# Expert units of two mixture-of-experts layers as side work of the state space block between them

## The chip, the cores and the metric

The kernel runs on one NeuronCore of a Trainium2 chip. The core has TensorE (PE, with its weight loads shown as PEld), VectorE (DVE), ScalarE (ACT), GpSimd (POOL) and SyncE (SP), each with its own in-order stream of instructions, and 16 DMA engines. The metric is device time in microseconds, the median of repeated runs; one further execution is profiled.

## The reference

4096 tokens of width 256 (two sequences of 2048) pass through three residual steps: a half-weighted expert layer, a state space block, and the same expert layer again.

```python
x = x + 0.5 * ffn(layernorm(x))      # 8 experts, top 2, capacity 640 per choice
x = x + attn(layernorm(x))           # Mamba block, then a squared-ReLU MLP
x = x + 0.5 * ffn(layernorm(x))      # the same weights again
```

The expert layer routes every token to its two best experts out of eight. For each of the two choices a token's position in its expert's queue is the running count over all tokens before it, and positions from 640 on are dropped. The expert is two matrix products (256 to 1024, ReLU, 1024 to 256), and the result is weighted by the gate probability and added to the token.

The Mamba block projects to 512 channels, convolves over four tokens, and then runs the recurrence `h = h*exp(dt*A) + dt*u*B` with 16 states for each channel along all 2048 tokens. Its output is `y = sum over states of h*C, plus x_conv*D`, multiplied by `silu(z)` and projected back to 256. All of it is float32.

## The kernel before

**Three stages one after the other.** `moe1` (L697) routes all 32 token tiles of 128 in five groups (`route`, L303), stores the normalized rows with their two gates in DRAM (`self.rows`), and copies x to `self.acc`. `experts` (L684) stores the list of token numbers per expert (`store_list`, L495), cuts every expert's kept tokens into units of 256 slots (`plan`, L504), and runs 32 of these (`units`, L570). If the plan holds more than 32, a branch runs seven more. `mamba` (L1095) is the middle stage, and `moe2` (L726) is `experts` again on the block's output, whose routing was done inside the middle stage.

**A unit.** It fetches 256 token numbers, then their rows, by indirect DMA on POOL's queue (L589, L600), and the expert's weights (L609) unless the buffer three units back holds the same expert. PE transposes the rows (4 transposes, L621), runs 16 matmuls into the hidden layer (L640, 256 columns each) and 16 out of it (L656). ACT does ReLU with bias, DVE adds the second bias and multiplies by the gate, and two indirect DMAs add the 256 rows to `acc` or `out` (L662).

**The middle stage.** The tokens are cut in 8 chunks of 512, the channels in 4 blocks of 128, taken in 2 pairs. `recurrence` (L928) is a hand-written order of 8 x 2 x 16 x 2 = 512 slots (chunk, pair, state, block of the pair). In a slot ACT makes the decay (`dA`, L969), DVE scans 512 tokens (L979) and multiplies by C (L989), and PE adds the product into `y_ps` by a matmul with the identity (L994). POOL makes the input term `db` for both blocks of a pair at once (L961, 128x1024). B and C rows come broadcast by DMA (`bt`, `ct`, L949 and L950), one pair ahead. After the 16 states of a pair, `gate` (L996) adds x_conv*D on DVE (L1002) and multiplies by silu(z) on POOL (L1006).

**Side chains.** What a chunk needs before its slots (`chunk_front`, L735: norm, projections, convolution, softplus) and after them (`chunk_tail`, L1026: projection out, MLP, dispatch to experts) are Python generators. Each `yield Need(...)` announces the next step with a cost for each engine, a PSUM bank, and marks to wait for. `Side` (L70) keeps a running clock of each engine's work; after each slot it puts in those steps that fit (`slot`, L141), and before a step of the main order that needs a mark it forces the steps that lead to it (`until`, L155). All of it is decided when the program is built; on the chip each engine runs its stream in that order.

Of the kernel before, what the change touches and what calls it, by code (L numbers as in the profile page):

```python
# [35 lines left out]
NU = K2 * NT // UN  # L36
MU = NU + E - 1
NWB = 3
W_2 = ND * FF
W_B1 = W_2 + NF * D  # L40
W_B2 = W_B1 + NF
# [9 lines left out]
XB = 4  # L51
PR = 2
NP = NC // PR
GROUPS = (4, 4, 8, 8, 8)
# [3 lines left out]
class Need:  # L58
# [4 lines left out]
    def __init__(self, pe=0.0, act=0.0, dve=0.0, pool=0.0, bank=0, free=0, after=None, sets=None):  # L63
        us = {"pe": pe, "act": act, "dve": dve, "pool": pool}
        self.us = {e: t for e, t in us.items() if t}
        self.bank, self.free, self.sets = int(bank), free, sets
        self.after = None if after is None or after[1] < 0 else after


class Side:  # L70
# [6 lines left out]
    OWN = {"dve": 1.8, "act": 0.88, "pe": 0.88, "pool": 1.25}  # L77
# [9 lines left out]
    def begin(self, chain, at=0.0):  # L87
        self.chains.append([chain, None, at])
        self.advance(self.chains[-1])
# [9 lines left out]
    def advance(self, chain):  # L99
        need = next(chain[0], None)  # L100
        while need is not None and not isinstance(need, Need):
            self.begin(need, chain[2])
            need = next(chain[0], None)
        chain[1] = need
        if need is None:
            self.chains.remove(chain)

# [9 lines left out]
    def step(self, chain):  # L117
# [8 lines left out]
        if need.sets:  # L126
            self.mark(need.sets, end)
# [27 lines left out]
    def until(self, mark):  # L155

        while mark[1] >= 0 and mark not in self.marks:
            self.step(min(filter(self.may, self.chains), key=lambda c: self.start(c)[1]))


class Kernel:
# [6 lines left out]
    def setup(self):  # L168
        nc, ins = self.nc, self.ins
        cp = self.ctx.enter_context(self.tc.tile_pool(name="const", bufs=1))  # L170
        self.cpool = self.ctx.enter_context(self.tc.tile_pool(name="count", bufs=2))
        dp = self.ctx.enter_context(self.tc.tile_pool(name="scratch", bufs=1, space=DRAM))
# [32 lines left out]
        self.need = const([P, K2 * CAP // UN], "need")  # L205
        nc.gpsimd.iota(self.need, pattern=[[UN, K2 * CAP // UN]], base=0, channel_multiplier=0,
# [29 lines left out]
        none = const([1, 1], "none_i", I32)  # L236
        nc.gpsimd.memset(none, NT)

# [24 lines left out]
        for c in range(NC):  # L263
            for k in range(DC):
                nc.vector.tensor_scalar_mul(
                    self.taps[:, c, k, :], self.ident, self.half[:, c, k : k + 1]
                )
        self.minus = const([P, 1], "minus")
# [12 lines left out]
        self.rows = dp.tile([NT + 1, RW], F32, tag="rows", name="rows")  # L281
        row = const([1, RW], "none")
        nc.gpsimd.memset(row, 0.0)
        nc.sync.dma_start(out=self.rows[NT:, :], in_=row)
        self.lists = [dp.tile([NULL + 1, 1], I32, tag=f"list{i}", name="lists") for i in range(2)]
        for t in self.lists:
            nc.sync.dma_start(out=t[NULL:, :], in_=none)
# [15 lines left out]
    def route(self, x, t0, pool, bank):  # L303

        nc = self.nc
        n = x.shape[1]
        W, W3, Q = [P, n, E], [P, n, K2], K2 * E
        num = self.exp_m8.unsqueeze(1).to_broadcast(W)

        def t(name, shape=W, dtype=F32, **kw):  # L310
            return pool.tile(shape, dtype, tag=f"r_{name}", name=name, **kw)
# [25 lines left out]
        lg = t("lg")  # L337
        for j0 in range(0, n, 4):
# [22 lines left out]
            for j in range(4):  # L361
# [5 lines left out]
                lg[:, j0 : j0 + 4, :], lq, self.gb.unsqueeze(1).to_broadcast([P, 4, E]), ALU.add  # L367
            )

# [50 lines left out]
        g1 = row[:, :, D]  # L420
        nc.vector.scalar_tensor_tensor(g1, e2, 0.5, rden, ALU.mult, ALU.mult)
        nc.vector.scalar_tensor_tensor(row[:, :, D + 1], rden, 0.5, g1, ALU.mult, ALU.subtract)
# [30 lines left out]
        nc.vector.tensor_tensor(at, at, late, ALU.add)  # L453
        yield Need(dve=1.6)

        WO, WN = [P, n, K2, P], [P, n, K2, E * PB]
# [20 lines left out]
        ll = psum("ll", [P, K2, 2, E * PB])  # L477
# [12 lines left out]
        nc.sync.dma_start(out=self.tiles(self.rows[:NT, :], n)[t0 // n], in_=row)  # L490
# [4 lines left out]
    def store_list(self, pool, ps, to):  # L495

        nc, n = self.nc, K2 * E * PB
        lp = ps.tile([P, P], F32, tag="lists", name="lists")[:n, :]
        nc.tensor.transpose(lp, self.list.rearrange("p c b -> p (c b)"), self.ident)
        lt = pool.tile([P, P], I32, tag="p_list", name="lt")[:n, :]  # L500
        nc.vector.tensor_copy(lt, lp)
        nc.sync.dma_start(out=to[:NULL, :].rearrange("(b p) o -> b (p o)", p=P), in_=lt)

    def plan(self, pool):  # L504
# [3 lines left out]
        nc = self.nc  # L508
        v = nc.vector
        WE, WB = [P, MU, E], [P, MU, UB]  # L510
        nn = K2 * CAP // UN

        def t(name, shape, dtype=F32):
            return pool.tile(shape, dtype, tag=f"p_{name}", name=name)

        kept, ks = t("kept", [P, K2 * E]), t("ks", [P, E])
        v.tensor_scalar_min(kept, self.count, float(CAP))
        k0 = kept[:, :E]
        v.tensor_tensor(ks, k0, kept[:, E:], ALU.add)
        more, nu, cu, cx = t("more", [P, E, nn]), t("nu", [P, E]), t("cu", [P, E]), t("cx", [P, E])  # L520
        v.tensor_tensor(
            more, ks.unsqueeze(2).to_broadcast([P, E, nn]),
            self.need.unsqueeze(1).to_broadcast([P, E, nn]), ALU.is_gt,
        )
        v.tensor_reduce(nu, more, AX.X, ALU.add)
        v.tensor_tensor_scan(cu, self.ones[:, :E], nu, 0.0, ALU.mult, ALU.add)
        v.tensor_tensor(cx, cu, nu, ALU.subtract)
        past, inn = t("past", WE), t("inn", WE)
        un = self.unum.unsqueeze(2).to_broadcast(WE)
# [657 lines left out]
```

## Time and profile before

| | us |
|---|---|
| median of 3 runs | 2442.43 (2440.75 to 2444.05) |
| profiled execution | 2459.16 |
| its span | 2457.4 |
| first expert matmul, stage one | 117.9 |
| first and last scan | 667.5, 1892.2 |
| first expert matmul, stage two | 1983.4 |
| mean granted TensorE clock | 0.914 |

| engine | busy us | share |
|---|---|---|
| PE | 2051.3 | 83% |
| PEld | 1296.4 | 53% |
| DVE | 1386.9 | 56% |
| ACT | 1029.3 | 42% |
| POOL | 1441.5 | 59% |

Times inside the profile count from the start of the span. The page lists groups of instructions as "line engine operation output<-inputs, shape, count | busy us, mean ns | idle before, and what ended it". A busy share over the whole span mixes three stages with different limits, so the stages are read one by one: the table of stretches gives each engine's busy time between two times. A float32 matmul is recorded twice (two passes), so 512 y matmuls appear as 1024.

### The profile page before, as it was taken

How to read it: one execution, taken by the hardware profiler on the slowest of the kernel's cores; microseconds unless marked ns; L12 is line 12 of the kernel's file. 1: busy time of each engine (PE TensorE's matmuls, PEld its weight loads, DVE VectorE, ACT ScalarE, POOL GpSimd, SP SyncE). 2: the span in 40 equal slices, each digit the busy share in tenths (PEclk: the TensorE clock that was granted, in tenths of full speed). 3: DMA queues.
4: the chain of work that ended last, by engine and by line, in shares of the span. 5: the costliest groups of instructions: out<-in, count | busy, mean ns of one | idle time of the engine just before them, and what ended most of it. 6: DMA issues, size and time to landing. Idle time of an engine off the chain costs nothing. (4 is left out here: it accounts for less than half of the span.)

```text
span 2457.4 us, 23707 instructions
## 1 busy us (share of the span) xinstructions
PE 2051.3 (83%) x7196; PEld 1296.4 (53%) x7196; DVE 1386.9 (56%) x2358; ACT 1029.3 (42%) x2307; POOL 1441.5 (59%) x1145
## 2 busy tenths in 40 slices
PE   3499999997687977979889698798686469999998
PEld 1288888885232433424334243243232258888887
DVE  5611111111298989989999899899998301111111
ACT  3122222222467675665756557557343212222222
POOL 2355555642478776675866767668554155556553
PEclk7699999998799988989989899798787779999999
DMA  8145454461133433334434334334342225454463
GB/s 312 62 139 143 117 172 113 114 180 18 57 123 127 121 120 110 121 96 130 142 100 129 102 121 137 94 121 120 111 127 75 108 82 168 121 146 125 131 183 97
DMA packets 141791, 302.00 MB, mean 123 GB/s; under 512 B 24447, under 2 KB 65174, under 8 KB 135638
## 3 DMA queue, kind: packets, MB, share of 16 engines
q1 hardware_dynamic: 103766, 176.50, 23.0%
q0 software_dynamic: 37888, 123.88, 18.2%
q8 instruction: 62, 1.02, 0.2%
q14 instruction: 75, 0.61, 0.1%
HBM read 318.85 MB, written 34.23 MB: 144 GB/s over the span
## 5 line engine op out<-in xcount | busy, mean ns | idle before, releaser
L994 PE MATMUL y_ps<-hc,ident 128*128 128x512 f32 x1024 | 588.8, 676 | 212.3 <-DVE hc L989 200.3
L961 POOL TENSOR_TENSOR db<-dtu,bt 128x1024 f32<-128x1024 f32 x256 | 601.7, 2358 | 207.1 <-DVE h L979 173.8
L645 ACT ACTIVATE h<-hp,w 128x256 f32<-128x256 f32 x512 | 215.0, 471 | 779.3 <-issue 501.7
L979 DVE TENSOR_TENSOR_SCAN h<-dA,st,db 128x512 f32<-128x512 f32 x384 | 494.6, 1288 | 32.3 <-ACT dA L969 3.8
L656 PE MATMUL yp<-w,h 128*128 128x256 f32 x2048 | 457.4, 382 | 10.1 <-issue 10.1
L994 PEld LDWEIGHTS y_ps<-hc,ident 128*128 128x128 f32 x1024 | 184.1, 202 | 531.9 <-DVE hc L989 399.9
L640 PE MATMUL hp<-xbT,w 128*128 128x256 f32 x2048 | 457.5, 382 | 1.6 <-DVE xbT L625 1.6
L640 PEld LDWEIGHTS hp<-xbT,w 128*128 128x128 f32 x2048 | 392.4, 192 | 56.6 <-DVE xbT L625 2.4
L656 PEld LDWEIGHTS yp<-w,h 128*128 128x128 f32 x2048 | 387.1, 192 | 61.7 <-issue 10.9
L969 ACT ACTIVATE dA<-dt,A 128x512 f32<-128x512 f32 x512 | 357.4, 699 | 0.3
L989 DVE TENSOR_TENSOR hc<-h,ct 128x512 f32<-128x512 f32 x512 | 345.1, 674 | 4.7 <-ACT st L984 4.7
L625 DVE COPY xbT<-tp 128x512 f32<-128x512 f32 x64 | 44.3, 692 | 463.6 <-PE tp L621 383.9
L984 ACT COPY st<-h 128x1 f32<-128x1 f32 x512 | 80.7, 158 | 402.9 <-DVE h L979 401.1
L660 DVE TENSOR_TENSOR y<-yp,w 128x256 f32<-128x256 f32 x128 | 54.4, 425 | 340.9 <-PE yp L656 340.9
L662 POOL DMA_INDIRECT acc<-y,ids x64 | 102.5, 1602 | 165.6 <-PE hp L640 76.9
L662 POOL DMA_INDIRECT out<-y,ids x64 | 102.2, 1597 | 165.5 <-DVE y L661 72.1
L979 DVE TENSOR_TENSOR_SCAN h<-dA,db 128x512 f32<-128x512 f32 x128 | 157.1, 1228 | 31.6 <-POOL db L961 17.9
L589 POOL DMA_INDIRECT ids<-lists,idx x128 | 128.5, 1004 | 70.8 <-issue 70.8
L600 POOL DMA_INDIRECT xb<-rows,ids x128 | 130.7, 1021 | 39.0 <-issue 39.0
L909 PE MATMUL in_ps<-rT,w_in 128*128 128x512 f32 x256 | 127.6, 624 | 7.0 <-ACT xpad L794 5.6
L801 PE MATMUL cv_ps<-xpad,taps 128*128 128x512 f32 x256 | 122.2, 603 | 0.1
L909 PEld LDWEIGHTS in_ps<-rT,w_in 128*128 128x128 f32 x256 | 50.2, 200 | 72.9 <-issue 48.1
(199 smaller groups left out, 1944.8 us busy)
## 6 DMA issues: line engine op xcount, KB each, us to landing
bt<-bc SPq DMA_DIRECT2D x256, 256.0 KB, 3.6
ct<-bc SPq DMA_DIRECT2D x256, 256.0 KB, 3.4
w<-in_expert SPq DMA_DIRECT2D x6, 2180.0 KB, 12.8
rows<-row SPq DMA_DIRECT2D x10, 516.0 KB, 6.5
x<-in_x SPq DMA_DIRECT2D x8, 512.0 KB, 8.8
acc<-x SPq DMA_DIRECT2D x8, 512.0 KB, 7.6
x<-acc SPq DMA_DIRECT2D x8, 512.0 KB, 4.9
out<-x SPq DMA_DIRECT2D x8, 512.0 KB, 3.6
```

Source lines behind the costliest of these rows:

```text
L589: nc.gpsimd.indirect_dma_start(out=ids[u][:, j : j + 1], out_offset=None, in_=lists[:, :], in_offset=bass.IndirectOffsetOnAxis(ap=idx[:, u ...
L600: nc.gpsimd.indirect_dma_start(out=xb[u][:, j, :], out_offset=None, in_=self.rows[:, :], in_offset=bass.IndirectOffsetOnAxis(ap=ids[u][:, ...
L640: nc.tensor.matmul(hp[:, q, :], lhsT=w1[:, k, (f + q) * P : (f + q + 1) * P], rhs=xT[u][:, k, :], start=(k == 0), stop=(k == ND - 1),)
L645: nc.scalar.activation(h[:, f + q, :], hp[:, q, :], AF.Relu, bias=b1[:, f + q : f + q + 1])
L656: nc.tensor.matmul(yp, lhsT=h[:, f, j * P : (j + 1) * P], rhs=w2[:, f, :], start=(f == 0), stop=(f == NF - 1),)
L662: nc.gpsimd.indirect_dma_start(out=acc[:, :], out_offset=bass.IndirectOffsetOnAxis(ap=ids[u][:, j : j + 1], axis=0), in_=y[:, j, :], in_of ...
L909: self.nc.tensor.matmul(mp, lhsT=self.w_in[:, k, m * P : (m + 1) * P], rhs=rT[:, k, :], start=(k == 0), stop=(k == ND - 1),)
L961: nc.gpsimd.tensor_tensor(db[n], chunks[i]["dtu"][c // PR], bt[n].unsqueeze(1).to_broadcast(WP), ALU.mult)
L969: nc.scalar.activation(dA[k], chunks[i]["dt"][c], AF.Exp, scale=self.A[:, c, s : s + 1])
L979: nc.vector.tensor_tensor_scan(h[k], dA.pop(k), db[k // PR][:, k % PR, :], chunks[i - 1]["state"][:, c, s : s + 1] if i % (T // TC) else 0 ...
L989: nc.vector.tensor_tensor(hc, h.pop(k), ct[k // PR], ALU.mult)
L994: nc.tensor.matmul(y[c], lhsT=self.ident, rhs=hc, start=(s == 0), stop=(s == DS - 1))
```

## The change

21 of the 64 units leave the expert stages and become side chains of the middle stage.

- The first expert stage runs 22 units (`NU_A`), the second 21 (`NU_D`). Ten units of the first layer (`NU_B`) and eleven of the second (`NU_C`) are run by a new generator `spread_units`. The ten are planned so that they hold tokens of the second half of the sequence only (chunks 4 to 7), so the first four chunks need not wait for them. The eleven are full units of first-half tokens of the second layer, planned by `plan_half` once chunk 3 is routed. `plan` now knows, for each expert, the counts at the half and at the end; `plan_rest` makes the list of the last 21. If the counts don't fit these sizes, a branch runs the rest up to 39, as before.
- A side unit has one buffer for the first weights (`wa`, loaded again once the hidden layer is done) and one for the second (`wb`); the weights lie in DRAM in two arrays, and the stages fetch them in two gathers per unit as well.
- While the recurrence has not begun, and after it, side units borrow its PSUM banks (`lone`, `lent`).
- The dispatch at a chunk's end keeps logits, and the part from top-2 on runs once for two chunks (`pair`). The rows are stored in two parts (values, then gates), and for the first four chunks also into a copy that the eleven units read.
- `db` is made for one block at a time (128x512), three slots ahead instead of a pair two pairs ahead; x_conv*D becomes a matmul with a diagonal matrix (`skip`) that opens the sum in `y_ps`, and the gate a single DVE multiply.
- The input x of a chunk is loaded twice (front and tail), and several buffers shrink (xc 8 to 6, dt 6 to 4, zs 6 to 4, dtu 3 to 2).
- At the start only one copy of the first expert's weights is loaded, where there were three; in the second stage it is loaded during the last tail.
- `Side`: costs of a slot are now DVE 1.95, PE 0 with every y matmul counted by itself at 0.88; chains have a rank, and a step may have a delay (`late`) for a transfer to land.

```diff
-NU = K2 * NT // UN
+NU_A, NU_B, NU_C, NU_D = 22, 10, 11, 21
+XC = 6
...
-    OWN = {"dve": 1.8, "act": 0.88, "pe": 0.88, "pool": 1.25}
+    OWN = {"dve": 1.95, "act": 0.88, "pe": 0.0, "pool": 1.27}
...
+    def spread_units(self, feed, m0, acc, last, pool, name, slots, known):
...
+        for u, slot in enumerate(slots):
+            yield Need(after=("slot", slot))
+            if u == 0:
+                yield from turn(0)
+            if u + 1 < n:
+                yield Need(pool=2.1, sets=(name + "ids", u + 1), late=3.0)
+                feed.ids_of(u + 1)
+            h = pool.tile([P, NF, UN], F32, tag="e_h", name="e_h")
+            for f in range(0, NF, 2):
+                lone = self.lone
+                yield Need(pe=1.8, bank=not lone, after=at("wa", u))
+                ps, tag = self.bank(lone)
+                hp = ps.tile([P, 2, UN], F32, tag=tag, name="e_hp")
+                self.into_hidden(hp, f, w1, xT[u])
...
+            if u + 1 < n:
+                yield Need(pool=1.0, sets=(name + "wa", u + 1), late=9.0)
+                feed.params_of(u + 1, wa)
+                yield from turn(u + 1)
+            lone = self.lone
+            for j in range(UB):
+                yield Need(pe=3.6, bank=j == 0 and not lone, after=at("wb", u))
...
+                self.from_hidden(yp[:, j, :], j, w2, h)
...
-                db[n] = sp.tile(WP, F32, tag="db", name="db", bufs=3)
-                nc.gpsimd.tensor_tensor(
-                    db[n], chunks[i]["dtu"][c // PR], bt[n].unsqueeze(1).to_broadcast(WP), ALU.mult
-                )
+                db[k] = sp.tile(W1, F32, tag="db", name="db", bufs=4)
+                nc.gpsimd.tensor_tensor(db[k], chunks[i]["dtu"][c // PR][:, q, :], bt[n], ALU.mult)
...
-            hc = sp.tile(W1, F32, tag="hc", name="hc", bufs=4)
-            nc.vector.tensor_tensor(hc, h.pop(k), ct[k // PR], ALU.mult)
+            t = hc[k] = sp.tile(W1, F32, tag="hc", name="hc", bufs=5)
+            nc.vector.tensor_tensor(t, h.pop(k), ct[k // PR], ALU.mult)
...
+                nc.tensor.matmul(
+                    y[c], lhsT=self.skip[:, c, :], rhs=chunks[i]["xc"][c], start=True, stop=False
+                )
...
-            nc.vector.scalar_tensor_tensor(
-                yc, ch["xc"][c], self.chan[:, c, DC + 1 : DC + 2], y[c], ALU.mult, ALU.add
-            )
             side.until(("z", NC * i + c))
-            nc.gpsimd.tensor_tensor(yc, yc, ch["zs"][c], ALU.mult)
+            nc.vector.tensor_tensor(yc, y[c], ch["zs"][c], ALU.mult)
...
+    def beside(self, pools):
+        chunk = NC * DS
+        slots = [chunk * (u - 4) // 2 for u in range(NU_B)]
+        acc = self.acc[:, :]
+        yield from self.spread_units(
+            self.feed_b, self.rest[1], acc, NT - 1, pools["exp"], "b", slots, True
+        )
+        yield Need(after=("planned", 0))
...
+        slots = [chunk * 4 + chunk * 4 * u // 14 for u in range(NU_C)]
```

## The prediction

> **What bounds the kernel now.** I read first the table of stretches, with the span cut at the stage borders that the timeline shows; its columns are stretch, length, busy us (instructions) of PE, PEld, DVE, ACT, POOL, then granted TensorE clock, DMA share and GB/s.
>
> ```profile
> core 0: us, PE busy (x) PEld busy (x) DVE busy (x) ACT busy (x) POOL busy (x), PEclk, DMA share, GB/s
> 667.00:1893.00 1226.00, 1002.90 (x2426) 428.20 (x2426) 1126.16 (x1499) 737.48 (x1648) 858.61 (x591) 0.91 0.39 118
> 1900.00:1985.00 85.00, 33.51 (x113) 19.77 (x112) 20.24 (x82) 13.87 (x30) 16.33 (x19) 0.67 0.25 95
> 590.00:667.00 77.00, 45.27 (x96) 18.52 (x96) 8.87 (x24) 29.06 (x49) 20.45 (x39) 0.77 0.12 35
> 179.00:585.00 406.00, 405.07 (x1930) 356.34 (x1928) 71.37 (x200) 94.06 (x224) 220.50 (x184) 1.00 0.48 133
> 2007.00:2437.00 430.00, 430.00 (x2053) 378.67 (x2052) 76.25 (x212) 101.05 (x241) 238.21 (x199) 1.00 0.52 145
> ```
>
> The two expert stages (last two rows) are PE alone, at clock 1.00. The recurrence between them is VectorE: 1126 of 1226 us. Two short serial stretches join them. The timeline of VectorE gives the price of a unit of 256 slots:
>
> ```profile
> 549.13 0.69 DVE L625 COPY xbT<-tp 128x512 f32<-128x512 f32 x1 [6.53 <-PE tp L621]
> ...
> 563.38 0.69 DVE L625 COPY xbT<-tp 128x512 f32<-128x512 f32 x1 [6.53 <-PE tp L621]
> ```
>
> One unit each 14.25 us. Then the costliest groups of the page, for the price of one of the 512 slots of the recurrence:
>
> ```profile
> L994 PE MATMUL y_ps<-hc,ident 128*128 128x512 f32 x1024 | 588.8, 676 | 212.3 <-DVE hc L989 200.3
> L961 POOL TENSOR_TENSOR db<-dtu,bt 128x1024 f32<-128x1024 f32 x256 | 601.7, 2358 | 207.1 <-DVE h L979 173.8
> L979 DVE TENSOR_TENSOR_SCAN h<-dA,st,db 128x512 f32<-128x512 f32 x384 | 494.6, 1288 | 32.3 <-ACT dA L969 3.8
> L989 DVE TENSOR_TENSOR hc<-h,ct 128x512 f32<-128x512 f32 x512 | 345.1, 674 | 4.7 <-ACT st L984 4.7
> ```
>
> VectorE needs 1.288 + 0.674 = 1.96 us a slot; the stage takes 1226/512 = 2.39. PE and POOL wait for VectorE (last columns). Where the other 0.43 goes: scan starts, read off the timeline, show that the first 32 slots of a chunk take 68 to 70 us, the last 32 take 83 to 92. The second kind holds the dispatch of the chunk before, and its groups (here 1344 to 1435 us) show tiny operations that take as long as POOL's db (2.36):
>
> ```profile
> L379 DVE TENSOR_SCALAR key<-sh 128x32 f32<-128x32 f32 x1 | 2.3, 2257 | 0.0
> L427 DVE COPY step<-count 128x16 f32<-128x16 f32 x1 | 2.0, 1971 | 0.0
> ```
>
> With POOL idle, at the end of the stage, the first takes 0.18:
>
> ```profile
> 1941.63 0.18 DVE L379 TENSOR_SCALAR key<-sh 128x32 f32<-128x32 f32 x1
> ```
>
> Last, two waits at the joints. In the waits of the first 120 us, ScalarE stands once for the store of the rows, which is queued behind 3 x 2180 KB of expert weights while DMA runs at 350 GB/s; and before the second expert stage POOL stands 13 us after the plan is done (1959.3) for the list, stored by SP behind three such loads:
>
> ```profile
> ACT row L333 <- DMA rows<-row: 20.8, 1, 20.8
> ```
>
> ```profile
> 1972.13 1.19 POOL L589 DMA_INDIRECT ids<-lists,idx  x1 [21.70 <-issue]
> ```
>
> **The change part by part.** The sum is made against the profiled execution, 2459.2 us (span 2457.4), which lies 16.7 above the median of 2442.4.
>
> Does it do what it says? From the reference's inputs I counted tokens per expert: 31 units in the first expert layer, 19 of them of the first half, and 32 in the second, of which 11 are full units of the first half. So 22 + 10 and 11 + 21 hold exactly, and the spare branch is not taken.
>
> *Taken out of the expert stages:* 10 and 11 units at 14.25: -142.5 and -156.8. POOL gets one gather more for each remaining unit (two weight parts): 1.3 us beside 7.7 (220.50 over 28.5 units), under 14.25, so PE stays the bound. Units 1 and 2 must now fetch their weights instead of finding them loaded; they land while units 0 and 1 compute, 0 to 10 us, I take +2.
>
> *First dispatch:* one weight load, issued after the first row store, instead of three before it. The 20.8 us wait should shrink to some 5; the copies of x still share the DMA, so I take -14 (0 to -18). The plan grows: its VectorE work from 97.57 to 105.5 is 8 us, of 312-element operations at 0.48; now five of 624 elements (0.75 each), a product and a sum over 2496 (2.65 each, at the same rate), some 40 small ones: about 18, +10. Sum -4.
>
> *Chunk 0's front* (590 to 667): in the built order of PE's instructions 2.4 units, 34 us, stand before the first y matmul, with their gathers and scatters on POOL between the softplus steps. PE is idle 32 of 77 us here, but a unit's group of 1.8 us ahead of a conv delays it. 0 to +34; +10, nearer the idle time.
>
> *The recurrence.* Between the first and last y matmul the built order holds 14.8 units. Work by instruction counts times the durations above (a 256-column matmul 0.427, from 14.25 us for 32 of them and 4 transposes; 512 columns 0.853):
> - PE: 861 before; + 14.8 x 14.25 = 211 + 32 skip matmuls 27, less what slips out at the end: 1093.
> - VectorE: per unit one copy 0.69 and one add 0.69, +20; plan of the half +12; 8 dispatches of about 30 small operations become 4, -30; the gate gains 0.06 x 32: 1101 before, 1102 after.
> - POOL: db 512 x 1.27 for 256 x 2.36, +48; yc x zs moves to VectorE in place of the D step, -41; 14.8 units of six gathers (1.0 and 0.3 to the next issue), two scatters (1.6 and 0.3) and two small gates, part of which falls outside, +157: 886 to 1050.
> - SP: row stores are split and doubled, and a second load of x per chunk stands in the same queue as bt and ct; they are prefetched a pair ahead (3.6 us landing, some 10 us lead): 0 while that lead holds, some us per chunk if not; bounds 0 to +25, taken 0 as 0.39 DMA share leaves room.
>
> So VectorE stays the longest, but PE comes within 1%. [...] By the row, PE is busy 1003 of 1226, and 238 more would not fit: 1241. [...] I count columns instead, and get 1093. Second, the clock: the row grants 0.91 over this stage, 1.00 in the expert stages; 1093/0.91 = 1201. [...] I take 0.95: 1150 on average.
>
> The average is not the path. Cut at 8 slots in the built order, VectorE has about 17 us, while PE has single stretches of 27 to 39 (slots 120, 152, 408 among them), where a whole unit's 16 output matmuls and a front meet. PE's queue is in order: behind them wait the y matmuls, and VectorE stops when its 5 hc buffers (some 10 us) are full. Summing the excess over those 10 us gives 16 to 20 us at full clock, 30 to 35 at 0.95, 60 to 72 at 0.9. POOL's lead is 3 slots; its excess sums to 1 to 10. Against it: the tiny operations lose about 46 us to db now (sum over their rows of mean less unhindered time); half as many, each standing behind at most 1.27 instead of 2.36: about 15 left, -30. Other dependencies tighten too (dt, zs, xc with fewer buffers), +10. Sum: 35 + 5 - 30 + 10 = +20, bounds -30 to +100.
>
> *After the recurrence* (scan end 1893.5 to the first matmul of the second stage 1983.4, 90 us): chunk 6's dispatch now ends here, +8; four units (57 us of PE) in the tail's gaps, PE idle 51 of 85 there, last one beside the list, ids and rows: +6; second dispatch half +4; larger plan +9; list no longer behind the loads, -11. Sum +16, bounds -5 to +50.
>
> Sum: -142.5 - 156.8 + 2 - 4 + 10 + 20 + 16 = -255; 2459.2 - 255 = 2204; less 16.7: **2187**.
>
> **The rivals.**
> 1. *PE becomes the bound of the recurrence.* For it: the bursts, and stretches that grant 0.82 to 0.89 in every second half-chunk. Against: those are the halves in which VectorE starves PE. With 0.9 the stage is +60 to +75 instead of +20: about 2237.
> 2. *Hidden better.* The waits at db vanish, units fit the gaps, joints cost nothing: recurrence -25, joints +5 instead of +26: about 2122.
> 3. *Slower: POOL waits for its own landings.* The ids must land before the rows, the first scatter before the second (the end of the chain shows 3.85 and 3.90 us for one). POOL is in order, so each wait holds the next db. Six waits of 4 us per unit would be 24 x 14.8 = 355 on top of 1050 = 1405, +179 in place of +20: 2346. The whole gain is eaten at +275, from 30.5 us of waits per unit (1501 = 1050 + 14.8 x 30.5); at 35, nine waits, it is 1568 and 2509. Against it: the steps of one unit are spread over 18 to 32 slots, 43 to 76 us, and the order puts other work between.
> 4. *The spare branch runs* (a routing that differs from my count): 17 or 18 units more, 2187 + 250 = 2437, no change; twice, slower.
>
> **How the numbers follow.** Likeliest 0.58 (2150 to 2225), rival 1 0.22 (2225 to 2275), rival 2 0.13 (2110 to 2150), rival 3 0.05 (0.02 of it slower), rival 4 0.02 (half each). From the edges of these I take 2130 to 2265, leaving out rival 3, rival 4 and the outer parts of 1 and 2. 0.2% is about what a measurement of this kernel can tell from no change. Faster 0.96, within 0.01, slower 0.03.
>
> **What would show it.** Expert stages at 14.25 per unit, PE 1.00, some 143 and 157 shorter. First matmul of the first stage near 114 instead of 117.9, with the 20.8 us wait gone. In the recurrence about 2.43 us a slot, VectorE above 0.88 busy, PE clock above 0.93, key<-sh at most 1.3. If VectorE's scan waits on db for more than 30 us in all, rival 3 is at work; if hc or y waits and a clock below 0.9 stand there, rival 1. I am wrong if the scan stage exceeds 1330 us or the joints together exceed 230 (now 167).

## The result and the profile after

The changed kernel takes 2430.36 us (median of 6 runs, 2427.19 to 2435.78) against 2442.09 (6 runs, 2438.01 to 2445.45): a ratio of 0.9957, 95% interval 0.9945 to 0.9968. I had forecast 2187 and a range from 2130 to 2265. The sign is right, but of the 255 us forecast 11.7 came.

The profiled execution after took 2435.03 us, its span 2433.3. Cut at the same borders as before, the table of stretches (stretch, length, busy us and instructions of PE, PEld, DVE, ACT, POOL, then granted clock, DMA share, GB/s) shows the scan stage, the stretch after it, the stretch ahead of it, and the two expert stages:

```profile
core 0: us, PE busy (x) PEld busy (x) DVE busy (x) ACT busy (x) POOL busy (x), PEclk, DMA share, GB/s
570.00:1954.00 1384.00, 1206.40 (x3448) 627.00 (x3449) 1103.45 (x1435) 777.16 (x1772) 1002.56 (x957) 0.95 0.51 129
1954.00:2099.00 145.00, 104.47 (x435) 79.17 (x433) 42.41 (x132) 36.98 (x84) 60.84 (x64) 0.86 0.31 83
459.00:570.00 111.00, 80.62 (x248) 48.94 (x248) 12.88 (x31) 38.11 (x72) 43.14 (x64) 0.85 0.20 54
115.00:459.00 344.00, 323.61 (x1492) 279.70 (x1492) 54.08 (x153) 73.90 (x176) 199.36 (x173) 0.97 0.58 170
2099.00:2416.00 317.00, 304.23 (x1424) 263.81 (x1424) 51.50 (x143) 70.52 (x168) 179.99 (x155) 0.99 0.58 173
```

VectorE's work in the scan stage has not grown (1126 before, 1103 now, in a stage 159 us longer), and TensorE is no longer busy all the time in the expert stages (323.61 of 344; it was 405.07 of 406). Between the borders, to a tenth:

| stretch | before | after | change | forecast |
|---|---|---|---|---|
| start to first expert matmul | 117.9 | 115.1 | -2.8 | -4 |
| first expert stage | 466.2 | 343.8 | -122.4 | -142.5 |
| to the first scan | 83.4 | 111.4 | +28.0 | +10 |
| first to last scan | 1224.8 | 1384.0 | +159.2 | +20 |
| to the first matmul of stage two | 91.2 | 144.9 | +53.7 | +16 |
| second expert stage and the end | 474.0 | 334.1 | -139.9 | -154.8 |
| span | 2457.4 | 2433.3 | -24.1 | -255 |

Of the 231 us by which the profiled spans miss the forecast, 139 lie in the scan stage, 56 at its two joints and 35 in the expert stages. The profiled execution before lies 17 us above the median of its kernel, the one after 5 us, which is why the table shows -24.1 and the medians -11.7; differences of some 10 us in a row of it are not safe.

The costliest groups of the page, and from the timeline the slowest of the three `key<-sh` of the scan stage, the small operation that stood behind POOL before:

```profile
L1368 POOL TENSOR_TENSOR db<-dtu,bt 128x512 f32<-128x512 f32 x512 | 653.0, 1321 | 190.8 <-DVE h L1384 90.5
L1405 PE MATMUL y_ps<-hc,ident 128*128 128x512 f32 x1024 | 546.7, 636 | 120.7 <-DVE hc L1394 119.5
L1384 DVE TENSOR_TENSOR_SCAN h<-dA,st,db 128x512 f32<-128x512 f32 x384 | 494.5, 1288 | 73.0 <-POOL db L1368 35.7
L1394 DVE TENSOR_TENSOR hc<-h,ct 128x512 f32<-128x512 f32 x512 | 344.7, 673 | 15.7 <-ACT st L1389 15.4
```

```profile
1125.21 1.16 DVE L490 TENSOR_SCALAR key<-sh 128x64 f32<-128x64 f32 x1
```

A scan and its product cost what they did (1.288 and 0.67). The small operation still takes about one db when it meets one, but db is half as long: 1.16 us beside db of 1.32, where before it took 2.26, 2.25 and 1.17; the other two now, and the other four before, took 0.18 to 0.19. What grew is time in which VectorE stands: 100 us of the stage before, 281 now. Its waits in the scan stage (total, times, longest):

```profile
DVE h L1384 <- POOL db L1368: 74.6, 45, 21.8
DVE v L1463 <- PE out_ps L1458: 45.0, 12, 6.0
DVE xc L1213 <- ACT th L1209: 25.4, 6, 8.1
DVE e_y L944 <- PE e_yp L843: 22.5, 12, 6.2
```

Only the first is a wait of the recurrence itself. The others are waits of side steps, and no scan runs while VectorE stands at one: around slot 160 its timeline has no scan between those at 975.45 and 1010.57, and shows such a place whole:

```profile
975.45 1.29 DVE L1384 TENSOR_TENSOR_SCAN h<-dA,st,db 128x512 f32<-128x512 f32 x1
976.65 0.67 DVE L1394 TENSOR_TENSOR hc<-h,ct 128x512 f32<-128x512 f32 x1
983.53 0.69 DVE L944 TENSOR_TENSOR e_y<-e_yp,wb 128x512 f32<-128x512 f32 x1 [6.22 <-PE e_yp L843]
989.40 0.69 DVE L1213 SCALAR_TENSOR_TENSOR xc<-th,cv_ps 128x512 f32<-128x512 f32 x1 [5.18 <-ACT th L1209]
990.35 0.19 DVE L467 TENSOR_TENSOR lg<-lq,gb 128x32 f32<-128x32 f32 x1 [0.26 <-PE lq L463]
998.67 0.69 DVE L1213 SCALAR_TENSOR_TENSOR xc<-th,cv_ps 128x512 f32<-128x512 f32 x1 [8.13 <-ACT th L1209]
1004.86 0.69 DVE L1463 TENSOR_TENSOR v<-v,out_ps 128x512 f32<-128x512 f32 x1 [5.51 <-PE out_ps L1458]
1009.37 0.69 DVE L1463 TENSOR_TENSOR v<-v,out_ps 128x512 f32<-128x512 f32 x1 [3.81 <-PE out_ps L1458]
1009.97 0.68 DVE L1414 TENSOR_TENSOR yc<-y_ps,zs 128x512 f32<-128x512 f32 x1
1010.57 1.28 DVE L1384 TENSOR_TENSOR_SCAN h<-dA,st,db 128x512 f32<-128x512 f32 x1
```

From 977.3 to 1010.6 VectorE works some 4 us and stands the rest, for six side steps that lie between two scans (the `yc` behind them is the recurrence's own gate). The reason is in the order as it was built. `gate` calls `side.until(("out", i - 1))` before it writes `yc`, since there are four `yc` buffers and the tail of the chunk before must have read them; if the planner has not placed that tail's projection by then, `until` places the earliest steps of all chains, one after another, ahead of the next scan. Between the first and the last slot it places 188 steps in this way (137 for `out`, at slots 160, 224, 288, 352, 416 and 480; 51 for `dt`, at 124 and 252). In the kernel before it placed none there. If I call the time between two scans, less the scan and its product, a gap, nine gaps over 5 us add up to 134 us after, and three to 21 us before. Seven of the nine lie right behind the slots just listed, all but 252: 18.6 us at 124, 33.2 at 160, 15.2 at 224, 5.5 at 288, 15.8 at 352, 22.3 at 416 and 12.4 at 480. In the one at 352 VectorE mostly works (the plan of the first half stands there in one piece), and so it does in the two gaps of 5.6 and 5.4 us that lie behind no deadline; in the others it mostly stands.

### The profile page after: what moved, and what is told of

It is laid out like the page before. It is cut to its first block, busy times and chain, and to the rows that moved or that the text cites. A ratio compares the mean times of both kernels' runs of the same rounds, so it can differ in the third digit from the quotient of the medians.

```text
span 2433.3 us, 24340 instructions
## 1 busy us (share of the span) xinstructions
PE 2063.3 (85%) x7253; PEld 1317.4 (54%) x7253; DVE 1342.2 (55%) x2234; ACT 1028.3 (42%) x2335; POOL 1520.0 (62%) x1481
## 5 line engine op out<-in xcount | busy, mean ns | idle before, releaser
L1368 POOL TENSOR_TENSOR db<-dtu,bt 128x512 f32<-128x512 f32 x512 | 653.0, 1321 | 190.8 <-DVE h L1384 90.5
L794 ACT ACTIVATE h<-hp,w 128x256 f32<-128x256 f32 x344 | 144.4, 471 | 564.6 <-PE hp L836 473.5
L836 PE MATMUL hp<-xbT,w 128*128 128x256 f32 x1376 | 308.0, 382 | 12.3 <-issue 11.5
L843 PE MATMUL yp<-w,h 128*128 128x256 f32 x1376 | 307.6, 382 | 0.0
L836 PEld LDWEIGHTS hp<-xbT,w 128*128 128x128 f32 x1376 | 264.0, 192 | 49.6 <-issue 11.9
L843 PEld LDWEIGHTS yp<-w,h 128*128 128x128 f32 x1376 | 260.9, 192 | 34.5
L836 PE MATMUL e_hp<-e_xT,wa 128*128 128x256 f32 x672 | 180.8, 419 | 15.2 <-DVE h L1384 7.1
L836 PEld LDWEIGHTS e_hp<-e_xT,wa 128*128 128x128 f32 x672 | 141.0, 213 | 70.6 <-issue 27.7
L843 PE MATMUL e_yp<-wb,e_h 128*128 128x256 f32 x672 | 152.9, 382 | 1.0 <-DVE xc L1213 1.0
L843 PEld LDWEIGHTS e_yp<-wb,e_h 128*128 128x128 f32 x672 | 128.6, 192 | 29.8 <-issue 10.8
L757 POOL DMA_INDIRECT acc<-y,ids x44 | 70.1, 1594 | 108.7 <-DMA acc<-y,ids 52.6
```

The lines of the kernel that those rows point to most:

```text
L757: self.nc.gpsimd.indirect_dma_start(out=dst, out_offset=bass.IndirectOffsetOnAxis(ap=ids, axis=0), in_=y, in_offset=None, bounds_check=las ...
L794: nc.scalar.activation(h[:, f + q, :], hp[:, q, :], AF.Relu, bias=b1[:, f + q : f + q + 1])
L836: self.nc.tensor.matmul(hp[:, q, :], lhsT=w1[:, k, (f + q) * P : (f + q + 1) * P], rhs=xT[:, k, :], start=(k == 0), stop=(k == ND - 1),)
L843: self.nc.tensor.matmul(yp, lhsT=h[:, f, j * P : (j + 1) * P], rhs=w2[:, f, :], start=(f == 0), stop=(f == NF - 1),)
L1368: nc.gpsimd.tensor_tensor(db[k], chunks[i]["dtu"][c // PR][:, q, :], bt[n], ALU.mult)
```

## The experiments

Three theories were tried on the scan stage: the two bt buffers (B), the load that the units put on TensorE (P) or on any engine (L), and the order (O); then one on the expert stages (Q). Runs 2 to 7 and 11 were timed once, so they have no interval. How far a stage moves by itself is seen from the scan stage of the same order in the changed kernel, run 1 and run 9: 1384, 1375 and 1375 us.

**1. Three bt buffers.** The change had also cut the `bt` buffers from three to two (`ct` got four), and SP stood 871 us at the bt load for a free one.

```diff
-                "bc": aside("bc", 2),
+                "bc": aside("bc", 3),
-                ct[n] = bcp.tile(W1, F32, tag="ct", name="ct", bufs=4)
+                ct[n] = bcp.tile(W1, F32, tag="ct", name="ct", bufs=3)
```

> The changed kernel with three bt buffers and three ct buffers, as before the change, in place of two and four; nothing else is edited. Theory B (a bt load can only be issued when the second db of the pair before last is done, lands 3.9 us later, and POOL cannot catch up after a burst of side work): VectorE's 75 us of scan waits on db in the recurrence fall to under 30, SP's wait for db at the bt load (871 us) disappears, the scan stage goes from 1385 to 1310-1345 us, the total to 2355-2390 us. Theory P (TensorE is late with the side chains' inputs, and VectorE stands at them in order; the db waits are its echo): scan stage within 15 us of 1385, total 2415-2435.

Measured: 2429.19 us, ratio to the kernel before 0.9955 (0.9941 to 0.9970), as the changed kernel itself. Scan stage 1375, waits for db 64.7 and not under 30. SP's wait for db at the bt load fell from 871 to 53 us, but since `ct` lost a buffer in the same edit its wait at the ct load rose from 79 to 1017. POOL's waits for bt loads fell from 83 to 49, and the time did not move. So a third bt buffer is worth nothing here, and B falls as it was put; P's figures (within 15 of 1385, 2415 to 2435) came out.

**2. No side units.**

```diff
-NU_A, NU_B, NU_C, NU_D = 22, 10, 11, 21
+NU_A, NU_B, NU_C, NU_D = 31, 0, 0, 32
...
-                side.begin(self.beside(pools), rank=4)
```

> The changed kernel with 31, 0, 0, 32 units: no unit beside the recurrence, all other edits kept (dispatch in pairs, D on TensorE, db per block, fewer buffers, split weights); the plan of the first half is not made. If the units are what made the recurrence longer: scan stage 1180-1230 us (1226 before the change), total 2400-2450. If the other edits did (buffers, db in halves, D on TensorE): scan stage over 1290, total over 2490. It also shows the pace of an expert unit with nearly every weight fetched: 14.25 us if the slower tail of the stages (15.0-16.2) comes from the units' hand-over, 15 or more after the ninth unit if it comes from fetching.

Measured: 2486.74 us, profiled span 2484.9. The scan stage, 1206, is inside the 1180 to 1230 expected; the total is 37 us above the 2400 to 2450, for the expert stages were slower than expected. The run splits the change in two. The edits other than units cost 27 us net by the profiles (span 2457.4 to 2484.9): the start gains 3 and the scan stage 19 (1206), and the expert stages lose 9 and 17, the joints 9 and 7, the end of the second stage 7. By medians they cost 46 (2486.74 against 2440.33 in the same session), for the profiled execution before lies above its median. The units gain 52 (2484.9 to 2433.3): 131 and 166 out of the expert stages, for 178 in the scan stage, 19 ahead of it and 47 behind it. The first stage has 31 units here and 32 before and, with the side units, after; at equal units the other edits cost one unit of some 14 us more, and the side units gain as much more. The run was also to tell where the slow pace of the expert stages comes from: here, too, a unit takes 14.25 us for nine units and then mostly 15 or more in the first stage, with no side unit to hand over to. So the pace belongs to the stage's own fetching (run 9). The scan stage of this kernel, in the same columns as above, and no gap over 5 us in it:

```profile
682.00:1889.00 1207.00, 1026.55 (x2471) 439.62 (x2470) 1074.02 (x1369) 719.82 (x1629) 859.34 (x815) 0.92 0.48 125
```

**3 to 5. The units with work cut out, in the same order.** First most of TensorE's products, then POOL's scatters and weight gathers, then both.

```diff
 # TensorE: one of 2 products of the first layer, one of 8 of the second
-                self.into_hidden(hp, f, w1, xT[u])
+                for q in range(2):
+                    nc.tensor.matmul(
+                        hp[:, q, :], lhsT=w1[:, 0, (f + q) * P : (f + q + 1) * P],
+                        rhs=xT[u][:, 0, :], start=True, stop=True,
+                    )
-                self.from_hidden(yp[:, j, :], j, w2, h)
+                nc.tensor.matmul(
+                    yp[:, j, :], lhsT=h[:, 0, j * P : (j + 1) * P], rhs=w2[:, 0, :],
+                    start=True, stop=True,
+                )
...
 # POOL
-                self.scatter_add(acc, feed.ids[u][:, j : j + 1], y[:, j, :], last)
...
-                feed.params_of(u + 1, wa)
...
-                feed.params_of(u + 1, wb)
```

> The changed kernel with most of TensorE's work taken out of the 21 side units (one of the 2 products of the first layer and one of the 8 of the second; so their output is not the expert's); the order of all other instructions stays, since the planner's costs stay. It takes about 10 us of TensorE from each unit. Theory P: the waits of VectorE for out_ps, e_yp, e_tp, pr_ps and lq in the recurrence (about 100 us) fall to under 40, the scan stage to 1260-1310, the start of the recurrence falls by some 20 us, total 2290-2350. Theory B: scan stage above 1350, total above 2380.

> The changed kernel without the scatters of the side units and without the weight gathers of their second and later units (their output is left out, and they use the first unit's weights): POOL loses four instructions a unit, DMA 2.2 MB of loads and 0.25 MB of adds. Theory B, with POOL's bursts as the cause of late db: db waits of VectorE under 30 us, scan stage 1290-1340, total 2310-2380. Theory P: scan stage within 25 us of 1385, total 2400-2430.

> The two cuts together: side units without most of TensorE's products, without scatters and without weight gathers after the first unit (their output is left out); the order of all other instructions is that of the changed kernel. A third theory now stands against both. Theory O (the order): it is written out when the kernel is built, by a planner with costs; in the changed kernel 188 steps of the recurrence are placed out of turn, all at once, because a deadline forces them (none before the change), and VectorE stands at each in order while no scan runs. Theory L (the load): the units' work on TensorE and POOL itself takes the time. Scan stage by O: 1310-1345 us, hardly under 1341 (without POOL's part) and 1359 (without TensorE's); by L: 1220-1270, since the kernel without units takes 1206.

Measured: 2380.81, 2379.41 and 2316.14 us. The scan stages:

| kernel | scan stage, us | gaps over 5 us, sum |
|---|---|---|
| changed | 1384 | 134 |
| less TensorE's part | 1359 | 123 |
| less POOL's part | 1341 | 114 |
| less both | 1306 | 109 |
| no units | 1206 | 0 |

```profile
557.00:1863.00 1306.00, 1093.98 (x2810) 498.37 (x2811) 1097.33 (x1436) 775.06 (x1772) 925.66 (x901) 0.94 0.45 119
```

Here, in run 5, TensorE has lost 112 us of work and POOL 77, and the stage is still 100 us longer than without units, with VectorE only 23 us busier (1097 against 1074).

- Run 3: P said 1260 to 1310 and is wrong; its waits for TensorE's products fell from 101 to 67 us, not under 40, and those for db rose to 83. The figures of B (above 1350, above 2380) came out.
- Run 4: P (within 25 of 1385) is wrong too. B's total came out (2310 to 2380), its stage missed 1340 by one, and VectorE's waits for db stay at 41.8, not under 30: late db is a part at most.
- Run 5: the stage lies between the theories, 4 us under O's 1310 to 1345 and 36 over L's 1220 to 1270.

Of the units' 178 us, TensorE's work carries 25 to 35 and POOL's with its transfers 43 to 54 (by which is taken out first), and 100 stay when both are gone. VectorE's own work is 23 of these. The gaps over 5 us are seven here, 109 us in all, and none without units. But run 5 alone does not part the order from what the emptied units still do (TensorE 67 us busier than without units, POOL 66, ScalarE 55); that takes runs in which the order alone changes, as 6 and 8.

**6 and 7. The same work, placed anew.** First the thin units with the planner told that they are thin, then all work with the planner told that units cost nothing.

```diff
 # 6, on top of 3
-                yield Need(pe=1.8, bank=not lone, after=at("wa", u))
+                yield Need(pe=0.9, bank=not lone, after=at("wa", u))
-                yield Need(pe=3.6, bank=j == 0 and not lone, after=at("wb", u))
+                yield Need(pe=0.45, bank=j == 0 and not lone, after=at("wb", u))
 # 7, in every Need of spread_units
-pe=0.62   pe=1.8   pe=3.6   pool=0.5 to 2.2
+pe=0.05   pe=0.1   pe=0.1   pool=0.05
```

> As the run without most of TensorE's products in the side units (scan stage 1359 us with the order kept; the units' output is not the expert's), but the planner is told so (0.9 in place of 1.8 us, 0.45 in place of 3.6), and places everything anew. Theory O: the scan stage falls to 1260-1310. Theory L: it stays within 25 us of 1359.

> All work of the changed kernel, but the planner believes that a side unit's TensorE and POOL steps cost almost nothing; it then places the state space block's own steps nearly as without units (14 forced steps in place of 188), and the units' steps early, between them. Theory O: scan stage 1270-1340, total 2320-2390. Theory L: the real work takes its time, scan stage 1370 or more, total 2415 or more.

Measured: 2323.88 and 2485.57 us. In run 6 the scan stage falls from 1359 to 1320, and the gaps over 5 us from 123 to 59: the same instructions with another order are 39 us faster, though not the 49 or more that O had said, and more than the 25 that L allowed. In run 7 the stage takes 1441, with 21 gaps of 5 to 10 us each (157 in all): O had said 1270 to 1340, and L's figures (1370 or more, 2415 or more) came out. A planner that takes the units for free places hardly a burst (14 forced steps), and the stage is the longest of all. So forced steps are not the measure by themselves: run 6 has 161 of them, counted in the same way, and half the gaps. The load must be booked, and O is not the whole truth.

**8. Another tolerance.** One number of the planner, all work kept.

```diff
-    BEHIND = {"dve": 0.6, "act": 1.2, "pe": 4.0, "pool": 4.0}
+    BEHIND = {"dve": 1.5, "act": 1.2, "pe": 4.0, "pool": 4.0}
```

> All work of the changed kernel; one number of the planner differs: VectorE may be booked 1.5 us behind the slot in place of 0.6. That leaves 93 forced steps of 188. Theory O: scan stage 1310-1350, total 2355-2395. Theory L: within 20 us of 1385 and of 2430.

Measured: 2398.57 us, ratio 0.983 (0.9813 to 0.9846). The scan stage (VectorE's work is the third figure, 1106 against 1103):

```profile
574.00:1904.00 1330.00, 1181.07 (x3397) 617.41 (x3397) 1106.43 (x1442) 767.71 (x1760) 995.40 (x949) 0.95 0.50 134
```

The largest gap is 11.7 in place of 33.2, and those over 5 us add up to 88. The stage is as O expected; the total is 4 us above O's range. With all work kept, order alone gains 54 us in the scan stage, of which 16 are given back after it (161 in place of 145). This is the part of the units' 178 us that is shown to be order.

**9. Rows between the scatters.** This is about the expert stages, where a unit takes 14.25 us for nine units and then mostly 15 to 16.2. POOL's timeline in the changed kernel, for the last scatter of one unit and the next unit, both of the slow kind:

```profile
389.93 1.57 POOL L757 DMA_INDIRECT acc<-y,ids  x1 [4.50 <-DMA acc<-y,ids]
391.81 1.07 POOL L197 DMA_INDIRECT xb<-rows,ids  x1 [0.30 <-issue]
393.19 1.04 POOL L197 DMA_INDIRECT xb<-rows,ids  x1 [0.30 <-issue]
394.54 0.99 POOL L197 DMA_INDIRECT w<-in_expert_in,widx  x1 [0.31 <-issue]
395.83 1.00 POOL L197 DMA_INDIRECT w<-in_expert_out,widx  x1 [0.30 <-issue]
397.13 1.61 POOL L757 DMA_INDIRECT acc<-y,ids  x1 [0.30 <-issue]
406.17 1.56 POOL L757 DMA_INDIRECT acc<-y,ids  x1 [7.42 <-issue]
```

and of the kernel before:

```profile
396.90 1.63 POOL L662 DMA_INDIRECT acc<-y,ids  x1 [1.45 <-DVE y L661]
401.55 1.58 POOL L662 DMA_INDIRECT acc<-y,ids  x1 [3.02 <-PE hp L640]
```

Before, POOL waited for VectorE's y (1.45): it had 1.4 us to spare in 14.25. After, it never waits for y at the first scatter (0.30): it is behind. The second scatter stands until the first has landed: 4.5 us in the first line, where the profile says so; by the table of waits it does so in 13 of the 22 units of the first stage, 52.6 us in all. The rows of the other two long waits name another releaser or none, but the semaphores in the trace tell the same: in the wait of 7.42 the last update from the first scatter comes at 405.40, and in the 3.02 of the kernel before at 400.77, each 0.77 or 0.78 us ahead of the second scatter, as in the waits that are named. The first scatter is issued closely behind 2.2 MB of weights (in the unit shown with nothing between), and lands after 5.4 and 8.3 us in the two units, against 3.9 before.

```diff
                 self.scatter_add(acc[:, :], ids[u][:, j : j + 1], y[:, j, :], NT - 1)
+                if j == 0 and u + NWB < hi:
+                    feed.rows_of(u + NWB)
```

> The changed kernel; in the two expert stages the two gathers of a unit's rows are issued between the two scatters of a unit, not after them. Theory Q (POOL's own queue sets the pace of the expert stages after the change: six gathers at 1.3 us, two scatters, and the second scatter standing until the first has landed make 15.5 us a unit, over TensorE's 14.25): the row gathers fill the wait, the pace falls to 14.25-14.6, the stages from 344 and 316 us to 322-332 and 298-308, the total to 2390-2410. Rival D (the DMA rate: nearly every unit now fetches 2.2 MB of weights, 171 GB/s in place of 133): the pace stays above 15, the total within 8 us of 2430.

Measured: 2377.65 us, ratio 0.9734 (0.9709 to 0.9758), 53 us under the changed kernel, more than Q's 20 to 40. Both stages run at 14.25 us for every unit (28.5 for two, without exception after the first), and take 315 and 301 us, 29 and 16 less (Q had said 322 to 332 and 298 to 308); in run 10, with the same edit, the DMA moves 186 and 176 GB/s there, more than the 170 and 173 of the changed kernel. In POOL's timeline the second scatter stands no longer:

```profile
375.24 1.62 POOL L757 DMA_INDIRECT acc<-y,ids  x1 [5.27 <-DVE y L806]
377.17 1.06 POOL L197 DMA_INDIRECT xb<-rows,ids  x1 [0.31 <-issue]
378.53 1.00 POOL L197 DMA_INDIRECT xb<-rows,ids  x1 [0.30 <-issue]
379.92 1.62 POOL L757 DMA_INDIRECT acc<-y,ids  x1 [0.39 <-issue]
```

Q is right in its cause and was too careful in its size; the DMA rate (D) is not it, and POOL has 5.27 us to spare.

**10. Six tolerances.** A setting that by the planner's own clock made the block 45 us shorter, on top of run 9.

```diff
-    BEHIND = {"dve": 0.6, "act": 1.2, "pe": 4.0, "pool": 4.0}
-    AHEAD = {"dve": 0.0, "act": 2.0, "pe": 4.5, "pool": 4.0}
-    EARLY = {"dve": 0.4, "act": 0.8, "pe": 1.0, "pool": 1.0}
+    BEHIND = {"dve": 2.5, "act": 2.0, "pe": 4.0, "pool": 4.0}
+    AHEAD = {"dve": 1.0, "act": 3.0, "pe": 4.5, "pool": 4.0}
+    EARLY = {"dve": 0.4, "act": 0.8, "pe": 2.0, "pool": 1.0}
-        yield Need(late=2.5, rank=1)
+        yield Need(late=2.5, rank=3)
```

> As the run before, and the planner's tolerances are changed at six places (VectorE may be booked 2.5 us behind and 1.0 ahead of the slot, ScalarE 2.0 behind and 3.0 ahead, TensorE's inputs may be ready 2.0 us after it, and the tail of a chunk has rank 3 at its start); all work of the changed kernel. By the planner's own clock the block is 45 us shorter. Theory O: scan stage 1310-1335 us, scan-free stretches over 5 us under 70 us in all (134 in the changed kernel), total 2345-2375. Theory L: scan stage above 1360, total above 2390.

Measured: 2374.5 us, ratio 0.9729 (0.9707 to 0.9752), but nothing over run 9: scan stage 1370 against 1375, gaps over 5 us 123 against 132. The expectation failed: its total came out only by what run 9 had gained, and of L's figures the stage (above 1360) did. The setting still forces 184 steps, 167 of them for `dt` and 13 for `out`; the planner's clock did not foresee the gaps.

**11. Thirteen side units.**

```diff
-NU_A, NU_B, NU_C, NU_D = 22, 10, 11, 21
+NU_A, NU_B, NU_C, NU_D = 26, 6, 7, 25
```

> The changed kernel with 26, 6, 7, 25 units: 13 side units in place of 21, nothing else edited; 72 forced steps in the recurrence in place of 188. Theory O: the last eight units cost more than an even share: scan stage 1285-1305 us, so that these eight save 124 us in the expert stages and cost 100 or more elsewhere, total 2430-2455. Were a side unit's cost even (10.3 us each in the scan stage, 2.4 at the joints), the stage would be 1302 as well, so it is the gaps without a scan that tell: by O they fall from 134 us to under 70.

Measured: 2450.31 us; scan stage 1307, gaps over 5 us 45, with 77 forced steps (five more than I had counted). Eight units more in the stages cost 121 us there and spare 77 in the scan stage and 36 after it: at the margin a side unit saves 15.1 us and costs 14.1. The gaps shrink by two thirds, as O said, but the stage by 77 us, where 8 of 21 even shares of the 178 are 68 and the expectation's 10.3 a unit gave 82. So this run does not show that the last units cost more than the others.

**12. Runs 8 and 9 together.**

> All work of the changed kernel, with the two edits that have gained alone: the row gathers between the scatters in the expert stages (gained 52 us) and VectorE booked up to 1.5 us behind the slot (gained 32). They act in different stages, so the gains should add up: total 2335-2365 us, expert stages at 14.25 us a unit, scan stage 1320-1345. If one only moved a wait that the other removes as well, the total would stay above 2370.

Measured: 2360.15 us, ratio 0.9642 (0.9625 to 0.9659), the fastest of all, 70 us under the changed kernel; the two gains alone add to 84. Scan stage 1334, expert stages 322 and 299; every unit after the first two of a stage takes 14.25, but the first of the first stage 17.6 in place of 9.9 in run 9, which is 7 of the 14 us that are missing.

## Why the prediction was wrong, point by point

- **Units out of the expert stages, -142.5 and -156.8 + 2.** Removing them was right, the price of those that stay was not. The failing step: "POOL gets one gather more for each remaining unit (two weight parts): 1.3 us beside 7.7 (220.50 over 28.5 units), under 14.25, so PE stays the bound." It added busy time only. The second scatter's wait of 3.0 us was there before; with it POOL had used 12.85 of 14.25, and the sum with one gather more leaves 0.1. With the scatter now closely behind the weights, the wait grew to 3.0 to 4.7 us, and 6.2 to 7.6 in four units of the first stage, and POOL fell behind. Run 2 has the slow pace without side units, and run 9 measures the mistake: 29 and 16 us.
- **First dispatch, -4.** Measured -2.8, which the table cannot tell from -4: kernels with the same start took 115 to 119 us to here. ScalarE's 20.8 us wait for the row store is 3.2.
- **Ahead of the first scan, +10, bounds 0 to +34.** Measured +28, inside the bounds: 9 without units, 19 by units; run 3 takes 12 of these off with TensorE's products.
- **The recurrence, +20, bounds -30 to +100.** Measured +159. The terms that are not units, -30 and +10, give -20, and run 2 measures -19 (not clear of the 17 us by which the profiled execution before lies above its median). The units were put at 35 + 5 = 40, and measured 178. The failing step is the one that turned their work into time: "Summing the excess over those 10 us gives 16 to 20 us at full clock, 30 to 35 at 0.95". It let five hc buffers cover 10 us of every TensorE burst. That can cover matmuls behind which only `y` waits. It does not cover side steps which stand in VectorE's own queue ahead of the next scan, and cutting the order at 8 slots hid these: six of them lie between two scans at slot 160, in an order that I had before me. In its place the runs show nine such gaps of 134 us (none without units), 54 us that come back by another order of the same work (run 8), 25 to 35 for TensorE's products and 43 to 54 for POOL's part with the order held. The sums of work did better, in part by luck: VectorE was forecast at 1102 and is busy 1103, but from the row's 1126 and not from the 1101 that the sum began with, and its terms add to +4 where it says +1; the small operations gained more than the 30 us put down for them (112 to 65 us). POOL was put at 1050 and is 1003. The clock, my estimate between the rows' 0.91 and 1.00, was put at 0.95 and came out so; it was halved 24 times in this stage (last section).
- **After the recurrence, +16, bounds -5 to +50.** Measured +54, outside the bounds: 7 without units, 47 by them. TensorE's busy time there rises from 38 to 104 us, so the tail of the units' work stands here and did not fit the gaps: the term of +6 for four units is the one that failed. Run 3 takes 21 off.
- **SP, 0 while the lead holds.** The lead does not always hold: POOL's db waits 83 us for bt loads (26 before, 74 without units). But run 1, where it waits 49, is no faster, so 0 is right as far as is shown.
- **The rivals.** Rival 1 (TensorE the bound) is 25 to 35 of the units' 178 us with the order held, and 64 where the planner may place the thinner units anew (run 6); its own sign, waits for y and a clock below 0.9, is absent (0.5 us, 0.95). Rival 2 (hidden better) did not come: waits at db grew from 17.9 to 74.6 us and the joints by 82. Rival 3 named the right wait in the wrong place: in the scan stage the waits put down to a scatter's landing are 3.2 us in all, while such waits set the pace of the expert stages. My sign for it, waits for db over 30 us, was no sign: it was met (74.6), but the kernel without units has 32.7 and one with POOL's part gone 41.8. Rival 4 did not happen; the spare branch did not run.
- **"I am wrong if the scan stage exceeds 1330 us or the joints together exceed 230."** 1384 and 256: both.

What stays open: how the 100 us that run 5 leaves divide between the order and the work of the emptied units, and why the planner lets the steps run into their deadlines. That it books TensorE as full is likely, as run 6 (lower cost, half the gaps) says, but the two PSUM banks that units and chunks share were not tried alone.

## What to carry to other kernels

When side work is woven into an in-order queue, do not sum it over windows: count what stands between two neighbouring instructions of the main chain, and price each at what it waits for. A deadline in a planner (`until`) turned lack of room into a stop of the main chain here, and the planner's own clock did not show it (run 10); to book the side work as free was worse still (run 7). POOL, which in the expert stages mostly issues transfers, had a cycle of its own, waits for landings included: 12.85 of a unit's 14.25 us before the change. Before a transfer is added to such a queue, look for the idle time that tells how much of the cycle is left.

## What the runs showed of the hardware

- The second scatter of a unit, to the same tensor as the first, stood until that had landed: in the first expert stage 2.9 to 4.3 us before the change, mostly 3.0; after it, with the first issued closely behind 2.2 MB of weights, 3.0 to 4.7 us, and 6.2 to 7.6 in four units. In run 9, with two gathers between, it stood 0.39 us in the unit shown.
- Small operations of VectorE that met POOL's db took up to about as long as that: in the scan stage key<-sh 2.26, 2.25 and 1.17 us before, with a db of 2.36 on average, and 1.16 after, for twice the elements, with one of 1.32; the others 0.18 and 0.19. All operations of at most 64 elements a partition in the scan stage took 112 us (335 of them) before and 65 (225) after.
- In the scan stage after, where the granted clock of TensorE was 0.95 on average, it was halved 24 times, for 3.4 to 23.9 us each. The times between its changes there were 3.41 us or multiples of that. In the 3.41 us ahead of a fall, for the 23 falls that have these within the stage, TensorE was busy 2.0 us or less, most often 1.0 to 1.5, and not at all in one; in stretches of the same length after which the clock stayed at 1.00 it was busy 1.5 us or more. One fall, in the columns of the first table:

```profile
1822.72:1826.13 3.41, 1.47 (x7) 0.62 (x6) 2.86 (x5) 0.52 (x2) 3.08 (x3) 1.00 0.95 123
1826.13:1829.54 3.41, 2.67 (x4) 1.50 (x5) 3.31 (x7) 0.75 (x2) 2.85 (x3) 0.50 0.41 67
```

- With SP's wait at the bt load cut from 871 to 53 us, and that at the ct load grown from 79 to 1017, the time was the same (2429.19 and 2430.36 us): neither wait set it.
